# A two-layer convolution block on one Trainium2 core: half of an image's statistics on another engine, small chains cut finer, and outputs one unit later

## The chip, the cores and the metric

The kernel runs on one core of a Trainium2 chip. A core has five engines that matter here, each with its own instruction stream that runs strictly in its own order: TensorE (PE in the profile, with its weight loads as PEld) for matmuls, VectorE (DVE), ScalarE (ACT) and GpSimd (POOL) for elementwise work, and SyncE (SP), which issues all DMAs of this kernel. Data lies in HBM, in the on-chip memory SBUF, or in PSUM, the banks that TensorE writes. The metric is the device time of one execution in microseconds.

## The reference, cut to what matters

The input x is (4, 64, 256, 256), four images of 64 channels. Two layers each add a branch to x. The first layer normalises x by groups (mean and variance of pairs of channels over a whole image) and runs a gated branch; the second normalises the new x and runs two 3x3 convolutions with batch norm.

```python
# layer 0: x = x + L0(gn(x))
h  = gelu(conv3x3(x, c1_w))
xa, k = split(conv1x1(h, c2_w))
xs = gelu(conv_vertical3(conv_horizontal3(xa)))
weights = softmax(xs.mean(axis=(2, 3)) @ gate_w.T)   # one gate per image
mask = the two largest of the three weights, else 0
out = xs
for i in range(3):                                    # ranks 2, 4, 8
    out = out + conv1x1(conv1x1(k, w2) * conv1x1(xs, w1), w3) * mask[i]
y = x + conv1x1(out, proj_w)
# layer 1: y + relu(bn(conv3x3(relu(bn(conv3x3(gn(y)))))) + gn(y))
```

Three things need a whole image before the next step can start: the group norm of x (statistics of x before the first convolution), the gate (the mean of xs before the outputs y), and the group norm of y (statistics of y before layer 1).

## The kernel before

**Tiling.** Two image rows share the 128 partitions with the 64 channels. An image is cut into 16 chunks of 16 rows. The first half of the kernel, the front, works on one chunk at a time; such a step is called a unit. There are 64 units for the four images (`UNITS`), and three more slots to finish. Unit u belongs to image u // 16. The front of a unit: the 3x3 convolution in a form that needs fewer products (differences of input rows on GpSimd and ScalarE, matmuls into the two banks ps_c, "butterflies" on VectorE at L610 to L629, gelu on ScalarE at L637), then the folded 1x1 and vertical taps (matmuls into ps_a, L641 to L671), their horizontal part on ScalarE and VectorE (L677, L683, L686, L689), gelu into xs (L705), the low-rank products (ps_k and ps_q, L712 to L746), and stores of xs and the low-rank product to HBM. ps_a has one bank, so the taps of a half unit must be taken out by L683 and L686 before the next taps may start. ps_c has two banks, freed by the two gelus L637.

**Other work in the units.** Beside the front of its own image, a unit also carries statistics of x of a later image, and outputs y of an earlier one.

- Statistics. A chunk of x is loaded (L403) and reduced. Image 0 is reduced before the units start: half of each chunk by VectorE (`stats_group`, L411, bn_stats over 512 values), half by ScalarE (`stats_piece`, L426: a piece is 1024 values, read twice, once with a shift and once squared, each pass leaving its sum). Images 1, 2 and 3 are reduced by ScalarE alone, two pieces a chunk: image 1 in units 1 to 11, image 2 in units 12 to 27, image 3 in units 28 to 43 (`plan_stats`). Then `stats_end` runs a chain of very small operations: sums on VectorE, a matmul that averages over channels, a mean, a second matmul, a square root on ScalarE, and so on.
- Gate. `gate(b)` is a chain of small operations: a sum, a matmul, a softmax over nine values with an exponential on ScalarE, the choice of the top two by comparisons on VectorE, and the weights `wm` and the bias that the outputs need.
- Outputs. For each of 32 octets of an image (two a unit): load xs, the low-rank product (`ranks`, every second chunk) and x, matmuls into ps_o (bank "p"), add (L848), bn_stats of y (L853), store y. `out_end` then ends the statistics of y with another small chain (L287 and `combine`).

**Order.** The order on all five engines is written out by hand. Each call is put at a step and an order number; `at_slot(u, pos, call)` puts it in slot u, where positions below 6 are its first step and positions from 6 on its second. All calls are then issued in that order. So a call with position 4.1 on VectorE comes after the butterflies of 4.05 and before the output's add (4.3) and L683 (5.2); on ScalarE, 1.52 comes after the second copy out of ps_c (1.4) and before the gelu L705 (1.55), and 4.45 after L677 (4.15). The chains are Python generators: each `yield` ends a part, and each place in a list runs the next part:

```python
e = NCH * b - 4
places = (e, 8.3), (e + 1, 1.25), (e + 1, 1.36), (e + 2, 1.25), (e + 2, 1.36), (e + 2, 1.52), (e + 2, 6.15), (e + 3, 1.25), (e + 3, 1.36)
chain = stats_end(b)
for place in places:
    at_slot(*place, next, chain, None)
```

For image b the gate stands in slots 16(b+1)+1 and 16(b+1)+2, and the outputs start at slot 16(b+1)+3 (`t` in `plan_out`) and take 16 slots: units 19 to 34, 35 to 50, and 51 to 61 for the 22 octets of image 2 that fit. The remaining octets, and all of image 3, are put into the second half, where layer 1's first convolution runs (`plan_out_late`). After that come the second convolution and a last pass that writes the result.

SP issues the DMAs in the same order: in a slot, first the input of a later unit (position 0), the `ranks` loads (0.2), the xs load (0.3), a chunk for the statistics (1.5), the x load for the outputs (2.0), stores of xs (4.7), of the low-rank product (8.1), of y (8.25) and of xs (8.6).

Of the kernel before, what the change touches and what calls it, by code (L numbers as in the profile page):

```python
# [41 lines left out]
def conv_preact_kernel(ctx: ExitStack, tc: tile.TileContext, io, col128, colset, col64):  # L42
# [219 lines left out]
    def combine(mv, n, avg, eps_t, out, name):  # L262
# [5 lines left out]
        nc.vector.tensor_reduce(mean, ps[:, 0:n], AX.X, ALU.add)  # L268
        nc.vector.tensor_scalar(mean, mean, 1.0 / n, None, ALU.mult)
# [155 lines left out]

    def stats_piece(b, n, i, at_sum=None):  # L426
# [29 lines left out]
    def stats_end(b):  # L456

        own = gn1[b] = stat.tile([P, 3], F32, tag="gn1", name=f"gn1_{b}")
        n = 2 if b == 0 else 1
        mv = stat.tile([P, n, 2], F32, tag=f"mv{n}", name=f"mv_x{b}")  # L460
        if b == 0:
            nc.vector.bn_aggr(mv[:, 1, :], flat(st_g.pop(b)))
# [289 lines left out]
    def gate(b):  # L752
# [11 lines left out]
        nc.vector.tensor_copy(lg, ps[:, 0:9])  # L764
        mx = stat.tile([P, 1], F32, tag="s2", name=f"mx_{b}")
# [14 lines left out]
        nc.vector.tensor_scalar(beat[:, 3:6], beat[:, 0:3], -1.0, 1.0, ALU.mult, ALU.add)  # L780
        keep = stat.tile([P, 3], F32, tag="keep", name=f"keep_{b}")
# [202 lines left out]
    with tc.manual_schedule(engines={mybir.EngineType.Activation}):  # L984
        for k in range(NCH):
# [3 lines left out]
            for i in range({0: 0, NCH - 1: 4}.get(k, 2)):  # L989
                stats_group(0, 2 * k - 2 + i if k else 0, k, i)  # L990
            for n in range({0: 2, NCH - 1: 0}.get(k, 1)):
                for i in range(2):
                    stats_piece(0, 2 * k + n if k == 0 else 2 * k + 1, i, k + n if k == 0 else k + 1)
# [13 lines left out]
        for _ in range(7):  # L1007
            next(first_end)
# [31 lines left out]
    def plan_front():  # L1040
# [54 lines left out]
        for b in range(B):  # L1095
            t = NCH * (b + 1)
            if b < B - 1:
                places = (t + 1, 8.3), (t + 2, 1.25), (t + 2, 1.36), (t + 2, 1.52), (t + 2, 6.15), (t + 2, 8.3), (t + 2, 9.06)
# [3 lines left out]
            else:  # L1102
                at_each(((CONV1 + 12 + n, 12.7) for n in (1, 3, 3, 4, 8, 12, 16)), gate(b))
# [11 lines left out]
    def plan_stats(b):  # L1115
# [4 lines left out]
        for k in range(NCH):  # L1120
# [418 lines left out]
```

## Time and profile before

| what | value |
|---|---|
| median of 6 runs | 3035.98 us (3031.72 to 3044.55) |
| profiled execution | 3038.26 us |
| its span in the profile | 3036.4 us |
| front, units 0 to 63 (first ps_c of unit 0 to the end of unit 63) | 63.8 to 1316.4 us |
| bn_stats of image 0 on VectorE, L414 | 32 of 685 ns mean |
| statistics passes on ScalarE, L432 | 112 of 1135 ns and 112 of 1053 ns mean |
| aggregate of y's statistics, L287 | 4 of 1883 ns mean |
| table load on ScalarE | 1283 ns each |

The profile is of one execution. PE, PEld, DVE, ACT, POOL and SP are the engines named above. L683 is line 683 of the kernel below. In a timeline, a row is a group of equal instructions with its start and its length, and in brackets the idle time of the engine before it and what ended it. A window gives for a stretch of time how long each engine was busy, the share of full speed that TensorE's clock was granted, and the share of time that the DMA engines were busy.

### The profile page before, as it was taken

The page shows a single profiled execution, that of the slowest core. Times are in us where ns is not written, and L with a number is a line of the kernel's source. Part 1 is how long each engine was busy: PE and PEld are TensorE (multiplying, and loading weights), DVE is VectorE, ACT ScalarE, POOL GpSimd, SP SyncE. Part 2 cuts the span into 40 slices and gives each one's busy share as a digit, 9 for nine tenths or more (in the row PEclk, how much of TensorE's full clock was granted, in tenths as well). Part 3 has the DMA queues.
Part 4 walks back from the last instruction along what each step waited for, and adds up shares of the span by engine and source line. Part 5 has one row for each costly group of instructions (what it writes and reads, how often), then busy time and mean ns, then how long its engine had stood idle before and what let it go on. Part 6 is the DMA issues. An engine that isn't in the chain of part 4 may idle for free.

```text
span 3036.4 us, 53036 instructions
## 1 busy us (share of the span) xinstructions
PE 2367.6 (78%) x21576; PEld 1506.4 (50%) x21576; DVE 2469.7 (81%) x2793; ACT 2053.7 (68%) x2274; POOL 1674.8 (55%) x1210
## 2 busy tenths in 40 slices
PE   1898899998999999978889999989999999100000
PEld 1444444444544445545556667767888888100000
DVE  5678688888888999968788888979998998876665
ACT  6898887786876555556566677878888888432222
POOL 5888887776777778734435555635555555000000
PEclk9999999999999999999999999999999999555555
DMA  8565479999999889849888898756777764899999
GB/s 343 190 242 223 189 253 369 349 348 344 327 342 328 295 286 326 294 151 319 311 321 334 335 337 324 267 206 234 256 274 262 266 241 139 332 415 421 425 427 411
DMA packets 135572, 915.35 MB, mean 301 GB/s; under 512 B 14944, under 2 KB 15712, under 8 KB 40608
## 3 DMA queue, kind: packets, MB, share of 16 engines
q1 hardware_dynamic: 135328, 911.97, 80.0%
q8 instruction: 169, 2.77, 0.4%
q14 instruction: 75, 0.61, 0.1%
HBM read 573.74 MB, written 338.17 MB: 300 GB/s over the span
## 4 chain that ended last, share of the span: by engine, by line
PE 26%; DMA 19%; DVE 6%; issue 2%; ACT 1%; POOL 1%; SPq 1%; DVEq 0%; POOLq 0%; ACTq 0%
PE ps_h L295 17%; PE ps_h2m L295 6%; DMA y_end<-y_d 5%; DMA out<-h 4%; DMA h<-h_d 4%; PE ps_hm L295 3%; DMA y<-in_xp 2%; DMA xs_in<-xs_d 2%; DVE h L317 1%; DMA yn<-y_d 1%; PE ps_o L492 1%; DVE diff L352 1%; POOL d L342 1%; DVE y L848 1%; DVE odd L361 1%
## 5 line engine op out<-in xcount | busy, mean ns | idle before, releaser
L295 PE MATMUL ps_h<-diff,w_q 128*128 128x512 f32 x3072 | 750.5, 399 | 10.4 <-DVE h L317 10.4
L295 PEld LDWEIGHTS ps_h<-diff,w_q 128*128 128x128 f32 x3072 | 576.4, 189 | 182.9 <-issue 27.2
L492 PE MATMUL ps_c<-v,us 64*64 64x256 f32 x9216 | 548.5, 387 | 41.8 <-DVE ps_c L623 35.8
L342 POOL TENSOR_TENSOR d<-yn 128x1024 f32<-128x1024 f32 x128 | 354.2, 2787 | 317.3 <-DMA yn<-y_d 187.9
L492 PEld LDWEIGHTS ps_c<-v,us 64*64 64x64 f32 x9216 | 363.8, 136 | 199.8 <-DVE ps_c L623 45.3
L492 PE MATMUL ps_a<-h,av 64*64 64x512 f32 x4080 | 389.9, 495 | 38.8 <-DVE t L686 28.6
L342 POOL TENSOR_TENSOR d<-h 128x1024 f32<-128x1024 f32 x127 | 311.8, 2476 | 194.8 <-DVE diff L350 133.3
L317 DVE SCALAR_TENSOR_TENSOR h<-ps_h,scale_w,m 128x1024 f32<-128x1024 f32 x256 | 323.5, 1279 | 65.8 <-PE ps_h L295 49.9
L540 POOL TENSOR_TENSOR x<-x 128x512 f32<-128x512 f32 x256 | 329.9, 1289 | 12.3
L1420 ACT ACTIVATE v<-y_end,shift,gn 128x2048 f32<-128x2048 f32 x64 | 133.8, 2093 | 281.8 <-DMA y_end<-y_d 246.6
L492 PEld LDWEIGHTS ps_a<-h,av 64*64 64x64 f32 x4080 | 155.9, 134 | 308.8 <-issue 204.7
L381 ACT ACTIVATE junk<-h,less_h 128x2048 bf16<-128x2048 f32 (+3 forms) x133 | 256.0, 1925 | 11.1 <-DVE h L317 11.0
L848 DVE SCALAR_TENSOR_TENSOR y<-ps_o,ob,y 128x1024 f32<-128x1024 f32 x128 | 163.8, 1280 | 121.4 <-DMA y<-in_xp 61.7
L1421 DVE SCALAR_TENSOR_TENSOR h<-h,ss,v 128x2048 f32<-128x2048 f32 x64 | 149.8, 2349 | 122.9 <-ACT v L1420 91.6
L683 DVE SCALAR_TENSOR_TENSOR t<-ps_a,m,t 128x1020 f32<-128x1020 f32 x128 | 163.3, 1276 | 104.6 <-ACT t L677 102.6
L677 ACT ACTIVATE t<-ps_a,tap_bias,m 128x1024 f32<-128x1024 f32 x128 | 154.0, 1203 | 103.1 <-PE ps_a L492 102.9
L705 ACT ACTIVATE xs<-t 128x1024 f32<-128x1024 f32 x128 | 134.8, 1054 | 122.6 <-DVE t L689 94.0
L295 PE MATMUL ps_h2m<-odd,w_q 128*128 128x512 f32 x768 | 192.7, 400 | 8.2 <-DVE odd L361 4.4
L295 PE MATMUL ps_hm<-odd,w_q 128*128 128x512 f32 x768 | 193.1, 400 | 4.2 <-ACT k L733 2.4
L352 DVE SCALAR_TENSOR_TENSOR diff<-d,gn,diff 128x1024 fp32r<-128x1024 f32 x128 | 192.1, 1530 | 4.5 <-ACT diff L345 4.5
L345 ACT ACTIVATE diff<-d 128x1024 fp32r<-128x1024 f32 x128 | 135.0, 1055 | 83.3 <-POOL d L342 82.1
L532 POOL TENSOR_TENSOR x<-x,x 128x512 f32<-128x512 f32 x128 | 160.7, 1277 | 43.3 <-ACT x L526 43.3
(226 smaller groups left out, 4322.8 us busy)
## 6 DMA issues: line engine op xcount, KB each, us to landing
h_d<-h SPq DMA_DIRECT2D x114, 1024.0 KB
x<-in_xc SPq DMA_DIRECT2D x64, 1280.0 KB
h<-h_d SPq DMA_DIRECT2D x64, 1152.0 KB
yn<-y_d SPq DMA_DIRECT2D x60, 1152.0 KB
xs_in<-in_xp SPq DMA_DIRECT2D x64, 1024.0 KB
xs_d<-xs SPq DMA_DIRECT2D x128, 512.0 KB
xs_in<-xs_d SPq DMA_DIRECT2D x64, 1024.0 KB
y<-in_xp SPq DMA_DIRECT2D x64, 1024.0 KB
```

Source lines behind the costliest of these rows:

```text
L295: nc.tensor.matmul(ps, wq[w][:, kind, kx, :], t[:, rows, kx : kx + W], start=(j == 0), stop=(j == len(terms) - 1))
L317: nc.vector.scalar_tensor_tensor(h.rearrange("p (e k) w -> p e (k w)", e=2), ps.rearrange("p e k w -> p e (k w)"), w_scale[w], m.unsqueeze ...
L342: engine.tensor_tensor(raw.rearrange("p (g r) w -> p g r w", g=2), *pair, ALU.subtract)
L352: nc.vector.scalar_tensor_tensor(lower, raw, scale, upper.bitcast(F32), ALU.mult, ALU.subtract)
L381: nc.scalar.activation(junk[rows, 0:n], flat(h), AF.Square, bias=less[name][rows], accum_out=total)
L492: last[:] = [nc.tensor.matmul(ps[o, at_out[0] : at_out[1], :], w[i], rhs[i], **flags)]
L532: nc.gpsimd.tensor_tensor(x4[:, j - 1], x_rows(u, j + 2), x4[:, j - 1], ALU.subtract)
L540: nc.gpsimd.tensor_tensor(x[:, r : r + 2], x[:, r + 2 : r + 4], x[:, r : r + 2], ALU.subtract)
L677: nc.scalar.activation(flat(t), flat(ps), AF.Identity, bias=tap_bias, scale=sh[:, 1:2])
L683: nc.vector.scalar_tensor_tensor(t[:, :, 1:W], ps[:, :, 0 : W - 1], sh[:, 0:1], t[:, :, 1:W], ALU.mult, ALU.add)
L848: nc.vector.scalar_tensor_tensor(y, ps.rearrange("p x s w -> p x (s w)"), out_bias[b], y, ALU.add, ALU.add)
L1421: nc.vector.scalar_tensor_tensor(h, h, ss2[:, 0:1], v, ALU.mult, ALU.add)
```

## The change

Four things change.

1. `HALVED = (0, 1)`: image 1's statistics are now split like image 0's. `stats_parts(k)` names for chunk k the groups for VectorE and the pieces for ScalarE. In all 32 bn_stats over 512 values go to VectorE, and 16 of the 32 pieces (two passes each) leave ScalarE. The groups stand at position 4.1 or 6.2 of slots 1 to 11.
2. `combine` has one more part (after its first reduction), and `gate` has two more (after the copy out of PSUM, and after the comparisons).
3. The places of these chains move. The gate's exponential moves from position 1.52 to 4.45, its later parts from 6.15, 8.3 and 9.06 of one slot to 6.05 of that slot and 4.1, 6.05 and 8.3 of the next. In `stats_end` the sums move from 8.3 to 4.1, the mean from 1.36 to 4.1 in part, the square root from 1.52 to 4.45, and the reciprocal from 6.15 to 8.3. `out_end` starts at position 4.1 of the slot after the last outputs instead of 8.3 of that last slot, and ends a slot later.
4. `plan_out` starts an image's outputs one slot later: `t` is 16(b+1)+4. Outputs now stand in units 20 to 35, 36 to 51 and 52 to 62.

The late chains in the second half get an extra place for the extra parts.

```diff
@@ combine
         nc.vector.tensor_reduce(mean, ps[:, 0:n], AX.X, ALU.add)
+        yield
         nc.vector.tensor_scalar(mean, mean, 1.0 / n, None, ALU.mult)
@@ stats
+    HALVED = (0, 1)
+
+    def stats_parts(k):
+
+        groups = [(2 * k - 2 + i if k else 0, k, i) for i in range({0: 0, NCH - 1: 4}.get(k, 2))]
+        pieces = [
+            (2 * k + n if k == 0 else 2 * k + 1, k + n if k == 0 else k + 1)
+            for n in range({0: 2, NCH - 1: 0}.get(k, 1))
+        ]
+        return groups, pieces
+
-        n = NCH if b == 0 else 2 * NCH
+        n = NCH if b in HALVED else 2 * NCH
...
-        n = 2 if b == 0 else 1
+        n = 2 if b in HALVED else 1
...
-        if b == 0:
+        if b in HALVED:
             nc.vector.bn_aggr(mv[:, 1, :], flat(st_g.pop(b)))
@@ gate
         nc.vector.tensor_copy(lg, ps[:, 0:9])
+        yield
         mx = stat.tile([P, 1], F32, tag="s2", name=f"mx_{b}")
...
         nc.vector.tensor_scalar(beat[:, 3:6], beat[:, 0:3], -1.0, 1.0, ALU.mult, ALU.add)
+        yield
         keep = stat.tile([P, 3], F32, tag="keep", name=f"keep_{b}")
@@ plan_front, the gate's places
-                places = (t + 1, 8.3), (t + 2, 1.25), (t + 2, 1.36), (t + 2, 1.52), (t + 2, 6.15), (t + 2, 8.3), (t + 2, 9.06)
+                places = (t + 1, 8.3), (t + 2, 1.25), (t + 2, 1.36), (t + 2, 4.1), (t + 2, 4.45), (t + 2, 6.05), (t + 3, 4.1), (t + 3, 6.05), (t + 3, 8.3)
@@ plan_stats
-            for i in range(2):
+            groups, pieces = stats_parts(k) if b in HALVED else ([], [(2 * k, None), (2 * k + 1, None)])
+            for i, (n, at_sum) in enumerate(pieces):
                 s = slots[k] + i * per / 2
                 first = s - int(s) < 0.5
                 for part in range(2):
-                    at_slot(int(s), ((4.35, 4.4) if first else (5.4, 9.15))[part], stats_piece, b, 2 * k + i, part)
+                    at_slot(int(s), ((4.35, 4.4) if first else (5.4, 9.15))[part], stats_piece, b, n, part, at_sum)
+            for group in groups:
+                s = slots[k] + group[2] // 2 * per / 2
+                at_slot(int(s), 4.1 if s - int(s) < 0.5 else 6.2, stats_group, b, *group)
         e = NCH * b - 4
-        places = (e, 8.3), (e + 1, 1.25), (e + 1, 1.36), (e + 2, 1.25), (e + 2, 1.36), (e + 2, 1.52), (e + 2, 6.15), (e + 3, 1.25), (e + 3, 1.36)
+        places = (e, 4.1), (e + 1, 1.25), (e + 1, 1.36), (e + 1, 4.1), (e + 2, 1.25), (e + 2, 1.36), (e + 2, 4.45), (e + 2, 8.3), (e + 3, 1.25), (e + 3, 1.36)
@@ plan_out
-        t = NCH * (b + 1) + 3
+        t = NCH * (b + 1) + 4
...
-            for place in ((e, 8.3), (e + 1, 1.25), (e + 1, 1.36), (e + 2, 1.25), (e + 2, 1.36), (e + 2, 1.52), (e + 2, 6.15)):
+            for place in ((e + 1, 4.1), (e + 2, 1.25), (e + 2, 1.36), (e + 2, 4.1), (e + 3, 1.25), (e + 3, 1.36), (e + 3, 4.45), (e + 3, 8.3)):
```

More of the change, by code (lines that the diff above doesn't have):

```diff
@@ L988, in conv_preact_kernel @@
                 stats_shift(0)
-            for i in range({0: 0, NCH - 1: 4}.get(k, 2)):
-                stats_group(0, 2 * k - 2 + i if k else 0, k, i)
-            for n in range({0: 2, NCH - 1: 0}.get(k, 1)):
+            groups, pieces = stats_parts(k)
+            for group in groups:
+                stats_group(0, *group)
+            for n, at_sum in pieces:
                 for i in range(2):
-                    stats_piece(0, 2 * k + n if k == 0 else 2 * k + 1, i, k + n if k == 0 else k + 1)
+                    stats_piece(0, n, i, at_sum)
             if k == 5:
@@ L1006, in conv_preact_kernel @@
         first_end = stats_end(0)
-        for _ in range(7):
+        for _ in range(8):
             next(first_end)
@@ L1102, in plan_front @@
             else:
-                at_each(((CONV1 + 12 + n, 12.7) for n in (1, 3, 3, 4, 8, 12, 16)), gate(b))
+                at_each(((CONV1 + 12 + n, 12.7) for n in (1, 3, 3, 3, 4, 8, 12, 12, 16)), gate(b))
         at_slot(1, 1.6, weights1_load)
@@ L1127, in plan_stats @@
                 for part in range(2):
-                    at_slot(int(s), ((4.35, 4.4) if first else (5.4, 9.15))[part], stats_piece, b, 2 * k + i, part)
+                    at_slot(int(s), ((4.35, 4.4) if first else (5.4, 9.15))[part], stats_piece, b, n, part, at_sum)
+            for group in groups:
+                s = slots[k] + group[2] // 2 * per / 2
+                at_slot(int(s), 4.1 if s - int(s) < 0.5 else 6.2, stats_group, b, *group)
         e = NCH * b - 4
-        places = (e, 8.3), (e + 1, 1.25), (e + 1, 1.36), (e + 2, 1.25), (e + 2, 1.36), (e + 2, 1.52), (e + 2, 6.15), (e + 3, 1.25), (e + 3, 1.36)
+        places = (e, 4.1), (e + 1, 1.25), (e + 1, 1.36), (e + 1, 4.1), (e + 2, 1.25), (e + 2, 1.36), (e + 2, 4.45), (e + 2, 8.3), (e + 3, 1.25), (e + 3, 1.36)
         chain = stats_end(b)
@@ L1220, in conv_preact_kernel @@
             if b == B - 2:
-                plan_out_late(b, range(22, NOCT), [CONV1 + 16 + 3 * n for n in range(10)], 13.6, [(CONV1 + n, 12.6) for n in (48, 50, 50, 52, 52, 52, 54)])
+                plan_out_late(b, range(22, NOCT), [CONV1 + 16 + 3 * n for n in range(10)], 13.6, [(CONV1 + n, 12.6) for n in (48, 50, 50, 50, 52, 52, 52, 54)])
         else:
@@ L1224, in conv_preact_kernel @@
             steps = [t + (e - 6 - t) * n // (NOCT - 1) for n in range(NOCT)]
-            plan_out_late(b, range(NOCT), steps, 13.6, [(e - i, 15) for i in (5, 3, 3, 1, 1, 1, -1)])
+            plan_out_late(b, range(NOCT), steps, 13.6, [(e - i, 15) for i in (5, 3, 3, 3, 1, 1, 1, -1)])
         plan_conv1(b)
```

## The prediction

> **What bounds the kernel now.** I read the page's totals first, then the TensorE timeline for a ruler, then windows cut at the units that the change touches, then timelines inside them. A unit is one of the 64 steps of the first half (63.8 to 1316.4 us); it starts where TensorE begins a run of 96 ps_c matmuls.
>
> ```profile
> PE 2367.6 (78%) x21576; PEld 1506.4 (50%) x21576; DVE 2469.7 (81%) x2793; ACT 2053.7 (68%) x2274; POOL 1674.8 (55%) x1210
> ```
>
> No engine is full over the whole, so the stages decide. Columns of the windows: us, busy time of PE, PEld, DVE, ACT, POOL, granted clock, DMA share, GB/s.
>
> ```profile
> 100.88:282.91 182.03, 162.18 (x2326) 85.80 (x2330) 134.87 (x163) 168.53 (x251) 154.47 (x141) 0.97 0.60 217
> ...
> 394.77:416.53 21.76, 17.93 (x249) 9.59 (x246) 18.22 (x28) 18.32 (x25) 17.03 (x16) 0.92 0.92 272
> ...
> 474.52:515.19 40.67, 37.91 (x533) 20.32 (x529) 33.35 (x42) 30.59 (x44) 30.68 (x29) 1.00 0.95 351
> ...
> 717.83:766.05 48.22, 42.05 (x538) 21.02 (x536) 43.88 (x69) 33.75 (x47) 30.65 (x29) 0.93 0.86 318
> 1041.86:1089.79 47.93, 41.48 (x535) 20.65 (x536) 43.64 (x69) 25.10 (x31) 29.63 (x29) 0.93 0.76 258
> ...
> 1128.87:1166.00 37.13, 37.04 (x532) 19.14 (x528) 33.53 (x42) 21.68 (x28) 30.37 (x29) 1.00 0.93 326
> 1277.42:1316.42 39.00, 32.73 (x468) 17.14 (x460) 28.63 (x34) 23.84 (x29) 19.48 (x21) 0.96 0.53 187
> 199.50:202.90 3.40, 3.40 (x40) 2.08 (x36) 3.33 (x3) 2.08 (x4) 2.34 (x3) 0.50 0.00 0
> ```
>
> The reader is to see three regimes. With outputs and no statistics (units 54, 55) TensorE is full: 37.13 a pair, my floor there. With outputs and a later image's statistics (units 21, 22) a pair takes 40.67 at a DMA share of 0.95: transfers bind, 3.5 above the floor. Without outputs (units 2 to 11) a unit takes 18.2, ScalarE busy 168.5 of 182. In units 34, 35 and 50, 51, where a gate chain meets a norm chain, the pair takes 48 and VectorE is busy 44 instead of 33.5.
>
> The floor without outputs is 17.2, between two starts in the TensorE timeline; the third line is a stall in the unit after:
>
> ```profile
> 171.31 5.36 PE L492 MATMUL ps_c<-v,us 64*64 64x256 f32 x96
> ...
> 188.53 5.40 PE L492 MATMUL ps_c<-v,us 64*64 64x256 f32 x96
> ...
> 199.17 4.51 PE L492 MATMUL ps_c<-v,us 64*64 64x256 f32 x48 [2.18 <-DVE ps_c L623]
> ```
>
> In that unit 7 (19.7 us to 208.24) ScalarE works off two statistics passes and `k` (L733, until 193.6) ahead of the copy L605, the butterflies come late, TensorE idles 2.18, and its clock is granted at 0.50 from 199.5 (last window): 48 matmuls take 4.51 instead of 2.82. The gap costs 2.18 + 1.69.
>
> **The change, term by term.** *Statistics of image 1.* ScalarE loses 16 pieces of two passes (1.13 + 1.04, start to start), 34.7 us over units 1 to 11. VectorE gains 32 bn_stats of 0.685 (row L414), 21.9. The gain lies between 0 and 182.0 - 10 x 17.2 = 10.0: units 8, 10 and 16 already stand at 17.2 under 4.7 to 6.9 of passes, so the floor is another chain (the single bank of ps_a: taps, L677, L683, L686, taps). Units 7, 9 and 11 hold most of it, by the cause just shown: I take 9.8. The price: in units 2, 3, 4, 5, 7, 9 and 11 two bn_stats (1.37) stand between L623 and L683. VectorE in unit 16, in unit 12, and in unit 34:
>
> ```profile
> 368.24 0.70 DVE L623 SCALAR_TENSOR_TENSOR ps_c<-d,ps_c 128x512 f32<-128x512 f32 x1
> 369.79 1.28 DVE L683 SCALAR_TENSOR_TENSOR t<-ps_a,m,t 128x1020 f32<-128x1020 f32 x1 [0.86 <-ACT t L677]
> ```
> ```profile
> 299.71 1.27 DVE L441 TENSOR_TENSOR st_sq<-st_sum 128x1 f32<-128x1 f32 x1
> ```
> ```profile
> 742.92 0.14 DVE L779 TENSOR_TENSOR beat<-gate 128x3 f32<-128x3 f32 x1
> 743.09 1.21 DVE L780 TENSOR_SCALAR beat<-beat 128x3 f32<-128x3 f32 x1
> ...
> 746.04 1.88 DVE L287 BATCH_NORM_AGGREGATE mv_y<-st_y 128x2 f32<-128x384 f32 x1
> ...
> 748.66 1.27 DVE L683 SCALAR_TENSOR_TENSOR t<-ps_a,m,t 128x1020 f32<-128x1020 f32 x1
> ```
>
> In unit 16 L683 waits 0.86 for L677, which hides that much of 1.37. Some 0.5 is left, and TensorE's next taps are queued behind L686. Bounds: 0.5 each (3.5) to 1.37 + 1.69 each (21.4), cover gone and clock lost. TensorE's idle there grows from 1.3 to 1.8; 1.32 (unit 6) kept the clock, 2.18 lost it, so I add 1.69 one time in five: 0.85 each, 5.9. The other groups stand behind L629, where VectorE idles 5.24 before 190.59: nothing; 1.37 each without that idle.
>
> *Sums of images 1 to 3, earlier in units 12, 28, 44.* Five small operations, 1.5 by mean rows, 3.5 with waits like 299.71 (298.85 to 302.33); image 1 adds an aggregate (1.02 for image 0, L462). Unit 12: 2.5 - 0.86 and the clock risk, 2.0 (1.0 to 5.3). Unit 44: 1.1. Unit 28: 0.3, the DMA wait of unit 29 covers the rest. GpSimd's edges get their mean a few us later, still a unit ahead.
>
> *Sqrt and Exp move from ahead of L677 to behind it.* With two table loads each is 1.28 + 0.29 + 1.28 = 2.85. Before, they are a 3.10 idle in unit 14 (341.44 - 319.77 = 21.67) and a 2.64 idle in unit 18 (21.76), clock lost in both. Behind L677 they delay L705 and the gelu L637, which frees the bank for the next ps_c. In unit 16 ScalarE idles 0.74 before L705 and the first L637 ends 1.21 before the next unit, so 2.85 - 0.74 - 1.21 = 0.9 is left (0 to 2.85). Unit 14: saves 4.4 to the floor, costs 1.6 (0.9 and the matmul of L276 with its wait, 0.7). Units 18 and 19 (40.2 against 34.4): save 5.8, cost 3.2 (Exp 0.9, L766 and L767 0.5, L779 and L780 0.7, the gate's matmul 0.4, clock risk 0.7). Units 46 and 52 lose 4.0 of such stall (20.79 and 20.33 against 18.57); units 44 to 46 get 2.5 back (1.1, Sqrt 0.9, a matmul), 52 to 54 get 2.9 (L287's 1.88 less 0.5 of cover, two matmuls 0.6, Sqrt 0.9), and 36 to 38 some 0.5, the DMA wait hiding the rest.
>
> *Gate and norm chains spread.* In unit 34 L779 to L799 and L287 are one block from 742.92 to 748.6 ahead of L683; TensorE idles 1.91 and 3.91 and loses the clock twice. Spread, a part is 0.4 to 1.9 against 0.4 to 1.5 of slack at its place. VectorE's sum bounds it below: 33.5 + the 6.9 of the gate that stays in units 50, 51 is 40.4, so 47.93 becomes 40.5 (gain 7.4; from 3, if all six parts cost TensorE 1.3, to 10.8, the floor). Units 34, 35 are held by transfers at 40.7: 48.22 becomes 41.7, 6.5.
>
> *Outputs one unit later.* Unit 19 loses them (counted in its floor), unit 62 gets them: TensorE's idle in units 62, 63 (1.62 and 2.48, both for L623) takes in the two blocks of 1.72, and 39.0 is already above the full pair's 37.13: nothing; 3.4 without that idle. The first differences of conv1 (1295.38) need an output tile whose store is now issued near 1278.8, 16 us of cover. On SP an output's loads and store move along, and the parity flips: two 256 KB loads of `ranks` leave the even slot, where they stand ahead of the `y` load that odd units wait for, and join the odd one. 0.5 MB at 351 GB/s is 1.4 us a pair, over 12 pairs (units 20 to 43) 17 either way. Odd units wait and even ones don't, so I take a small gain, 0.25 a pair: 3.0.
>
> **Sum.** Savings 9.8 + 4.4 + 5.8 + 7.5 (units 34, 35 to 40.7) + 10.8 + 4.0 + 3.0 = 45.3. Costs 5.9 + 2.0 + 1.6 + 3.2 + 0.3 + 1.0 + 3.4 + 0.5 + 2.5 + 2.9 = 23.3. Net minus 22. The profiled execution took 3038.26 (span 3036.4), 2.3 above the median of 3035.98; from the median, **3014 us**. Behind unit 63 only late chains are cut finer.
>
> A rule against the change. L441 took 1.27 above and 0.16 in most of its executions, 1.27 being a GpSimd operation (1.289, L540). The Trainium skill, "SBUF — State Buffer", section "Who interferes with whom", says that a VectorE operation with two SBUF inputs and a reading GpSimd operation exclude each other, the later one waiting out the other. By it each small two-input operation of the sums may wait so wherever it stands, 2 us more in units 12, 28 and 44 each: minus 16 instead of minus 22.
>
> **Rivals.** (A) The relief doesn't reach TensorE in units 2 to 11, and Sqrt and Exp cost as much behind L677: without 3.9, 2.8 and 2.6, minus 12.7, 3023. For it: units 8 and 10 are at the floor already. Against: unit 7's late copy. (B) The parity hurts: odd slots also hold the `low` store; a loss of 17 for the gain of 3 gives minus 2, 3034. For it: the DMA share of 0.95. Against: even units have slack. (C) The parity gives the full 17: 3000. (D) Slower: **VectorE work ahead of L683 becomes the bound.** 18 inserts stand there (7 statistics, 3 sums, 2 aggregates, 6 of gates). If each costs its length and a clock drop, 21.4 + 10.6 + 7.1 + 18.5 = 57.6, with 7 for the rest 64.6 against 45.3: 3055. It decides from 2.1 us an insert, (45.3 - 7) / 18; my sum has 0.9. For it: gaps of 1.62 and 1.91 lost the clock too. Against: the 0.86 that L683 waits.
>
> **How the numbers follow.** Forecast 0.50, own range 3004 to 3024; A 0.14, C 0.10, B 0.11, D 0.15. What a measurement of this kernel tells from no change is 0.2%, 6 us: faster 0.50 + 0.14 + 0.10 = 0.74, same 0.11 (B), slower 0.15 (D). The range 3000 to 3034 takes in C, A and B and leaves D out.
>
> **What would show it.** Units 50, 51 near 40.5 and 34, 35 near 41.7; units 7, 9, 11 under 18.5 at a clock of 1.00; no 3 us gap in units 14 and 18; the `y` wait of odd units shorter and not moved to even ones. Wrong: idle above 1.6 ahead of the ps_a taps in units 2 to 5, L683 right behind bn_stats with windows at 0.50.

## The result and the profile after

The changed kernel takes 3044.49 us in the median of 22 executions (3035.72 to 3057.84), the kernel before 3035.78 in the median of 45 beside it (3027.73 to 3050.56). The ratio is 1.0028, with a 95% interval of 1.0018 to 1.0037. It is slower by 0.3%, where 22 us less were forecast. The profiled execution took 3048.59 us, its span is 3046.8.

The totals by engine moved as the change meant them to: ScalarE 32 us down, VectorE 37 us up.

```profile
PE 2365.1 (78%) x21576; PEld 1497.2 (49%) x21576; DVE 2507.0 (82%) x2826; ACT 2021.3 (66%) x2210; POOL 1675.1 (55%) x1210
```

The windows of the changed kernel at the units that the prediction named: unit 7, units 12, 13, 14, unit 18, units 34 with 35, unit 36, units 50 with 51. The columns are those of the windows of before: us, busy time of PE, PEld, DVE, ACT, POOL, granted clock, DMA share, GB/s.

```profile
189.25:206.76 17.51, 15.64 (x228) 8.22 (x224) 14.88 (x21) 14.81 (x22) 15.53 (x15) 1.00 0.56 189
278.68:303.14 24.46, 19.04 (x244) 9.40 (x240) 21.31 (x30) 13.84 (x19) 17.03 (x16) 0.86 0.60 210
303.14:326.13 22.99, 17.83 (x231) 8.78 (x227) 15.67 (x20) 15.65 (x22) 16.47 (x16) 0.93 0.24 98
326.13:344.92 18.79, 16.39 (x247) 8.27 (x239) 12.21 (x18) 16.68 (x24) 14.55 (x15) 1.00 0.67 237
398.76:417.65 18.89, 16.50 (x250) 9.06 (x244) 16.47 (x24) 17.38 (x25) 16.26 (x16) 1.00 0.65 237
712.45:755.49 43.04, 39.25 (x534) 18.78 (x531) 39.57 (x58) 33.11 (x47) 30.59 (x29) 1.00 0.92 336
755.49:779.08 23.59, 20.62 (x277) 10.93 (x273) 22.74 (x28) 14.78 (x22) 14.96 (x14) 0.93 0.87 324
1037.63:1080.12 42.49, 39.18 (x533) 18.96 (x530) 40.68 (x58) 24.43 (x31) 30.64 (x29) 1.00 0.87 284
```

Unit 7 fell from 19.71 to 17.51 and keeps its clock. Unit 14 lost 2.9 (21.67 before), unit 18 2.9 (21.76), units 34 and 35 went from 48.22 to 43.04 and units 50 and 51 from 47.93 to 42.49. These are the gains that were sought, and they are there. But unit 12 grew from 17.28 to 24.46 and unit 13 from 19.58 to 22.99, with the clock down to 0.86 and 0.93, and unit 36 from 20.05 to 23.59.

**What happens in unit 12.** VectorE of the changed kernel there; in a timeline the columns are start, length, engine, line and operation, and in brackets the idle time before it and what ended it:

```profile
289.56 0.69 DVE L635 SCALAR_TENSOR_TENSOR ps_c<-d,ps_c 128x512 f32<-128x512 f32 x1
290.16 1.01 DVE L474 BATCH_NORM_AGGREGATE mv_x<-st_x 128x2 f32<-128x192 f32 x1
291.09 0.13 DVE L450 TENSOR_REDUCE st_sum<-st_acc 128x2 f32<-128x32 f32 x1
291.26 0.34 DVE L451 TENSOR_SCALAR st_sum<-st_sum 128x2 f32<-128x2 f32 x1
291.63 1.19 DVE L453 TENSOR_TENSOR st_sq<-st_sum 128x1 f32<-128x1 f32 x1
292.86 1.20 DVE L454 TENSOR_TENSOR mv_x<-st_sum,st_sq 128x1 f32<-128x1 f32 x1
293.98 0.14 DVE L455 TENSOR_TENSOR mv_x<-st_sum,shift 128x1 f32<-128x1 f32 x1
294.05 1.27 DVE L695 SCALAR_TENSOR_TENSOR t<-ps_a,m,t 128x1020 f32<-128x1020 f32 x1
```

GpSimd over the same time, and TensorE behind it:

```profile
290.30 1.27 POOL L582 TENSOR_TENSOR v<-x,e 128x512 f32<-128x512 f32 x1
291.53 2.51 POOL L544 TENSOR_TENSOR x<-x,x 128x512 f32<-128x512 f32 x2
```
```profile
286.09 4.07 PE L504 MATMUL ps_a<-h,av 64*64 64x512 f32 x24 [2.05 <-DVE t L698]
...
296.78 4.07 PE L504 MATMUL ps_a<-h,av 64*64 64x512 f32 x24 [3.13 <-DVE t L698]
```

The reader is to see five operations on one or two values per partition that take 3.0 us in all behind an aggregate of 1.01: 3.9 us from the start of the aggregate to that of L695 (L683 before). L453 and L454 take 1.19 and 1.20 where the same kind takes 0.14 in the row after them: each lasts until the GpSimd operation beside it is done. TensorE's next taps wait for L698, 3.13 us, and then run 24 matmuls in 4.07 instead of the 2.38 that they take at full clock. The earlier wait, 2.05 at the beginning of the unit, has another cause, shown in experiment 4. In unit 13 the mean part of the same chain does it again:

```profile
313.54 1.17 DVE L272 TENSOR_SCALAR d_x<-mv_x,gn 128x2 f32<-128x2 f32 x1
314.75 1.20 DVE L273 TENSOR_TENSOR d_x<-d_x 128x2 f32<-128x2 f32 x1
315.98 1.21 DVE L274 TENSOR_TENSOR d_x<-d_x,mv_x 128x2 f32<-128x2 f32 x1
```

L695 follows at 317.11, and TensorE idles 3.5 us.

**What the time is made of.** Unit 63 starts 4.8 us earlier than in the profile before (1291.6 against 1296.4), the last pass 2.6 us earlier (2598.9 against 2601.5), and yet the end is 10.4 us later: the last pass takes 447.9 us instead of 434.9. That pass issues the same transfers in both kernels. So the two profiles alone say neither that the front became slower nor why the median did, and this had to be settled first.

### The profile page after: what moved, and what is told of

Same layout as the page of the kernel before. It is cut to its first block, busy times and chain, and to the rows that moved or that the text cites. A ratio compares the mean times of both kernels' runs of the same rounds, so it can differ in the third digit from the quotient of the medians.

```text
span 3046.8 us, 53014 instructions
## 1 busy us (share of the span) xinstructions
PE 2365.1 (78%) x21576; PEld 1497.2 (49%) x21576; DVE 2507.0 (82%) x2826; ACT 2021.3 (66%) x2210; POOL 1675.1 (55%) x1210
## 4 chain that ended last, share of the span: by engine, by line
PE 27%; DMA 19%; DVE 5%; issue 2%; ACT 1%; SPq 1%; POOL 0%; DVEq 0%; ACTq 0%; POOLq 0%
PE ps_h L296 17%; PE ps_h2m L296 6%; DMA y_end<-y_d 5%; DMA out<-h 4%; DMA h<-h_d 4%; PE ps_hm L296 3%; DMA y<-in_xp 2%; DMA xs_in<-xs_d 2%; PE ps_o L504 1%; DVE h L318 1%; DVE diff L353 1%; DMA yn<-y_d 1%; DVE odd L362 1%; DVE y L862 1%; DMA y_d<-y 1%
## 5 line engine op out<-in xcount | busy, mean ns | idle before, releaser
L504 PE MATMUL ps_c<-v,us 64*64 64x256 f32 x9216 | 537.1, 382 | 36.3 <-DVE ps_c L635 26.3
L504 PEld LDWEIGHTS ps_c<-v,us 64*64 64x64 f32 x9216 | 354.7, 134 | 195.2 <-DVE ps_c L635 35.6
L862 DVE SCALAR_TENSOR_TENSOR y<-ps_o,ob,y 128x1024 f32<-128x1024 f32 x128 | 163.8, 1279 | 99.0 <-DMA y<-in_xp 55.0
L695 DVE SCALAR_TENSOR_TENSOR t<-ps_a,m,t 128x1020 f32<-128x1020 f32 x128 | 163.0, 1274 | 92.1 <-ACT t L689 91.0
L312 ACT ACTIVATE m<-ps_hm,m,scale_w 128x1024 f32<-128x1024 f32 x64 | 77.0, 1204 | 146.5 <-DVE h L318 95.5
```

Source lines behind the costliest of these rows:

```text
L504: last[:] = [nc.tensor.matmul(ps[o, at_out[0] : at_out[1], :], w[i], rhs[i], **flags)]
L695: nc.vector.scalar_tensor_tensor(t[:, :, 1:W], ps[:, :, 0 : W - 1], sh[:, 0:1], t[:, :, 1:W], ALU.mult, ALU.add)
L862: nc.vector.scalar_tensor_tensor(y, ps.rearrange("p x s w -> p x (s w)"), out_bias[b], y, ALU.add, ALU.add)
```

## The experiments

Medians and ratios to the kernel before, each measured beside it on one chip (with fewer loads one execution each, the changed kernel's on another chip):

| kernel | median us (executions) | kernel before, same chip | ratio (95%) |
|---|---|---|---|
| changed, again | 3042.94 (12) | 3036.69 | 1.0024 (1.0012 to 1.0036) |
| statistics half alone | 3039.24 (12) | 3036.69 | 1.0008 (0.9992 to 1.0025) |
| changed without the statistics half | 3033.38 (12) | 3036.69 | 0.9997 (0.9984 to 1.0010) |
| later outputs alone | 3036.94 (12) | 3036.69 | 1.0009 (0.9998 to 1.0021) |
| cut: before / changed | 2643.48 (4) / 2648.82 (4) | 3039.42 | |
| mended | 3029.27 (8) | 3039.42 | 0.9958 (0.9942 to 0.9974) |
| mended, statistics on ScalarE | 3030.29 (11) | 3037.93 | 0.9972 (0.9960 to 0.9984) |
| mended, gate moved too | 3027.60 (7) | 3037.93 | 0.9962 (0.9948 to 0.9976) |
| sums and means alone put back | 3032.12 (12) | 3037.53 | 0.9981 (0.9968 to 0.9994) |
| fewer loads: before / mended | 3029.65 / 3006.82 (1 each) | 3037.93 | |
| fewer loads: changed | 3027.79 (1) | 3037.53 | |

**1. The changed kernel again.** No edit.

> The changed kernel unaltered, profiled a second time. In its first profile unit 63 starts 4.8 us earlier than before the change, conv2 2.6 us earlier, and the last stage is 13 us longer (400 to 407 GB/s against 424 to 427, its large packets late in one cluster per step to the end). Theory SET (the change fixes the pace of the last stage, by what it does to the time at which the stage starts or to what runs ahead of it): the second profile shows the same, last stage 11 to 15 us longer than in the profile before, ratio 1.002 to 1.004. Theory DRAW (the pace of that stage is drawn anew in each execution, whatever the kernel): the stage comes out anywhere between the two lengths, and the ratio, a median over many executions, falls towards 0.999.

Its last pass took 434.4 us and started at 2601.0. Windows of the last pass, changed kernel, first profile and then second:

```profile
2900.00:2950.00 50.00, 0.00 (x0) 0.00 (x0) 31.85 (x14) 12.55 (x6) 0.00 (x0) 0.50 1.01 407
```
```profile
2900.00:2950.00 50.00, 0.00 (x0) 0.00 (x0) 32.19 (x14) 13.87 (x7) 0.00 (x0) 0.50 1.01 427
```

The DMA engines are full in both (1.01), at 407 GB/s in one execution and 427 in the other of the same program. So the pace of this pass is drawn in each execution, as DRAW said. But the ratio stayed at 1.0024, where DRAW expected 0.999: a second cause was missing.

**2. One part at a time.** The statistics half alone is the kernel before with the statistics of the change and nothing else:

```diff
-        if b == 0:
+        if b in HALVED:
             nc.vector.bn_aggr(mv[:, 1, :], flat(st_g.pop(b)))
...
+            for group in groups:
+                s = slots[k] + group[2] // 2 * per / 2
+                at_slot(int(s), 4.1 if s - int(s) < 0.5 else 6.2, stats_group, b, *group)
```

> The kernel before with the statistics half on VectorE alone; all chains and the outputs at their old places. Prediction's reading: units 2 to 11 lose 3 us (as the changed kernel does, not the 9.8 that I forecast), units 34 and 35 stay at about 48 and 50 and 51 at about 48; units 12 and 13 stay at 17.3 and 19.6 because the sums stand at their old place: the front ends 2 to 4 us earlier. SET with the statistics as its cause: the last stage is 11 us or more longer all the same, time 3042 to 3046, ratio 1.002 to 1.004. SET with another cause, or DRAW: last stage as before, 3032 to 3034, ratio 0.9985 to 0.9995.

The changed kernel without it:

```diff
-    HALVED = (0, 1)
+    HALVED = (0,)
```

> The changed kernel without the statistics half on VectorE: chains in more parts at their new places and outputs one unit later, ScalarE keeps all of the second image's statistics. Units 2 to 11 as before the change; units 12 and 13 still long (24 and 23) if the small VectorE operations ahead of L683 cost what they do by waiting for GpSimd, near 17 and 20 if it was the halved statistics that made them long; units 34 and 35 near 43, 50 and 51 near 42.5, so that the front ends about 2 us earlier than before. SET with the chains or the late outputs as its cause: last stage 11 to 15 us longer, ratio 1.002 to 1.004. DRAW, or the statistics as the cause: ratio 0.999 to 1.000.

The later outputs alone, put into the kernel before:

```diff
-        t = NCH * (b + 1) + 3
+        t = NCH * (b + 1) + 4
```

> The kernel before with the outputs of the first three images one unit later and nothing else; gate and norm chains at their old places, the end of the outputs moving with them. If the later outputs alone set units 34, 35, 50 and 51 free, these fall from 48 to 43 and 42.5 a pair, and the front ends about 10 us earlier; if the chains at new places did it, they stay at 48 and only the parity of units 20 to 31 changes, by 0 to 5 us in all. SET with the late outputs as its cause: last stage 11 to 15 us longer, ratio 1.001 to 1.003. Otherwise last stage as before and ratio 0.997 to 0.999.

Lengths of units, from the starts of the ps_c matmuls in each timeline (two profiles of the changed kernel agree within 0.2 in these units):

| units | before | changed | statistics alone | without statistics | later outputs alone |
|---|---|---|---|---|---|
| 2 to 11 | 182.0 | 178.9 | 178.9 | 181.9 | 183.6 |
| 12 | 17.28 | 24.46 | 21.21 | 23.86 | 17.28 |
| 13 | 19.58 | 22.98 | 19.57 | 21.68 | 19.60 |
| 14 | 21.67 | 18.79 | 21.48 | 18.79 | 21.68 |
| 18 and 19 | 40.2 | 38.2 | 40.1 | 38.2 | 39.0 |
| 34 and 35 | 48.2 | 43.0 | 48.2 | 42.5 | 46.7 |
| 50 and 51 | 47.9 | 42.5 | 47.9 | 42.5 | 47.8 |

Units 12 and 13 are long without the halved statistics too, so the chains did it; the halved statistics add 3.9 at unit 12 when they stand alone, which I had not expected at all. Units 34, 35, 50 and 51 were set free by the chains, not by the later outputs. The last passes took 435.8, 433.4 and 441.4, which again fits a draw and no part of the change: the later outputs, with the longest, have a ratio of 1.0009 whose interval holds 1. But the medians of two parts are not as expected: the statistics alone stand at 1.0008, between the ranges of DRAW and SET, with unit 63 no earlier than before (1297.7), and the later outputs alone at 1.0009, where 0.997 to 0.999 was expected. One thing stays open. Without the statistics half the changed kernel is 9.5 us faster in the median on the same chip (3033.38 against 3042.94), though its small operations stand where the changed kernel has them. Its profile shows unit 63 only 1.5 us earlier than the second profile of the changed kernel (1288.4 against 1289.9), but 7.8 earlier than the cut changed kernel of experiment 3 (1296.3), whose time is near its median; 5.7 of the 7.8 lie in units 20 to 33. With one profile of each it can't be told whether that is the price of the statistics half beside the chains or a difference between executions.

**3. The last pass taken away.** Front, both convolutions and 8 of 64 steps of the last pass remain:

```diff
-    steps = chunks[-KEEP:] + chunks[:-KEEP]
+    steps = chunks[-KEEP:][:8]
```

> The kernel before with its last stage ended after 8 of 64 steps: the other 56 outputs are not computed. What is left is the front, conv1, conv2 and 31 us of the last stage. Two theories of why the changed kernel's median is 6 to 9 us longer although its profiles reach the last stage earlier. TAIL: the front, conv1 and conv2 of the changed kernel are 1 to 4 us shorter also in the median, and the last stage is longer by 8 to 12 on average. HEAD: the one profile of the kernel before is a slow execution of its conv1, in the median its last stage starts at 2593 and not at 2601, and the last stage is drawn from the same lot for both kernels. Cut before: TAIL 2636 to 2640, its executions within 4 us; HEAD 2626 to 2631 with executions over 8 us or more.

> The changed kernel with its last stage ended after 8 of 64 steps: the other 56 outputs are not computed. TAIL: median 1 to 4 us below that of the kernel before cut the same way. HEAD: 5 to 9 us above it.

The changed kernel is 5.3 us longer (2648.82 against 2643.48), its executions 2646.0 to 2653.9 against 2643.2 to 2644.1. HEAD had the difference right (5 to 9) and its own account of the kernel before half wrong: that kernel's executions are not spread, they lie within 1 us, and its absolute time was 12 to 17 above what HEAD gave, 12 of which are my slip: the 8 steps that remain end after 43 us and not after 31. The rest of the whole kernels' time is the same: 3036.69 to 3039.42 less 2643.48 is 393 to 396 before, 3042.94 to 3044.49 less 2648.82 is 394 to 396 after. So most of the lost time lies ahead of the last pass, and the first pair of profiles misled: before's front was a long one (unit 63 at 1296.4, 1289.9 in the cut one), after's front a short one (1291.6; 1296.3 in the cut one, 6.3 later than the cut kernel before). This last pair, whose times are near their medians, is the one to take apart below.

**4. The chains put back.** The mended kernel:

```diff
-                at_slot(7 + 3 * i + n, 6.2, next, chain, None)
+                at_slot((7, 15)[i] + n, 6.2, next, chain, None)
...
-        places = (e, 4.1), (e + 1, 1.25), (e + 1, 1.36), (e + 1, 4.1), (e + 2, 1.25), ...
+        places = (e, 8.3), (e + 1, 1.25), (e + 1, 1.36), (e + 1, 1.36), (e + 2, 1.25), ...
...
-            for place in ((e + 1, 4.1), (e + 2, 1.25), (e + 2, 1.36), (e + 2, 4.1), (e + 3, 1.25), ...
+            for place in ((e + 1, 8.3), (e + 2, 1.25), (e + 2, 1.36), (e + 2, 1.36), (e + 3, 1.25), ...
```

> The changed kernel with its small VectorE chains taken from the place ahead of L695 to the places where they stood before: the sums and the output's aggregate at 8.3, the mean parts at 1.36 of the next unit; and the scaling of the w2 weights five units later, at units 15 to 17, so that the three long operations at unit 11 are not there beside the halved statistics. Theory PLACE (small VectorE operations ahead of L695 each wait for a running GpSimd operation and hold up units 12, 13, 36 and 52): unit 12 falls from 24.4 to 17.3 to 18.5, unit 13 from 23.0 to 19.6, units 36 and 52 from 23.3 to 20 to 21, the front ends 10 to 18 us earlier than before the change. Theory DATA (these units wait for something that moves with them, a load or the norm itself): they stay within 1 us of what the changed kernel has. The time: by HEAD 3028 to 3036, by TAIL 3020 to 3035.

Unit 12 fell to 17.21 and unit 13 to 19.59, as PLACE said; unit 52 fell to 21.6, where 20 to 21 was expected, and unit 36 stayed at 23.3: misses, taken up in experiment 6. At 3029.27 us (ratio 0.9958) it beats both kernels. The sums and means alone:

```diff
-        places = (e, 4.1), (e + 1, 1.25), (e + 1, 1.36), (e + 1, 4.1), (e + 2, 1.25), ...
+        places = (e, 8.3), (e + 1, 1.25), (e + 1, 1.36), (e + 1, 1.36), (e + 2, 1.25), ...
```

> The changed kernel with the sums and the mean part of the statistics chain alone back at their old places, 8.3 and 1.36 of the next unit; all else as changed. Theory PLACE: unit 12 falls from 24.4 to about 21.2 (what the halved statistics alone showed there, with the w2 scaling still at unit 11), unit 13 from 23.0 to 19.6, 6 to 7 us of the front; units 36 and 52 stay at 23.3. If that lead lasts to the end the time is 6 us below the changed kernel's, ratio 1.000 to 1.001 to the kernel before; if the transfers of units 20 to 44 take it back, ratio 1.001 to 1.0025.

Unit 12 took 21.22 and unit 13 19.58, just as expected, and the time fell more than expected: 0.9981, so that this one list of places turns the change from slower into slightly faster. The same three operations at their old place, VectorE in unit 13 of this kernel:

```profile
306.63 0.39 DVE L272 TENSOR_SCALAR d_x<-mv_x,gn 128x2 f32<-128x2 f32 x1
307.05 0.16 DVE L273 TENSOR_TENSOR d_x<-d_x 128x2 f32<-128x2 f32 x1
307.24 0.16 DVE L274 TENSOR_TENSOR d_x<-d_x,mv_x 128x2 f32<-128x2 f32 x1
```

They take 0.7 in all here and 3.6 in the changed kernel. What is left in unit 12 of this kernel, 4 us, stands at its beginning; VectorE from the end of unit 11 on:

```profile
277.12 1.56 DVE L253 TENSOR_SCALAR mset<-mset 128x768 f32<-128x768 f32 x1
278.72 1.50 DVE L254 TENSOR_SCALAR mset<-mset 128x768 f32<-128x768 f32 x1
280.14 1.27 DVE L415 BATCH_NORM_STATS2 st_x<-xs_in 128x6 f32<-128x512 f32 x2
...
282.52 0.68 DVE L420 BATCH_NORM_STATS2 first<-xs_in 128x6 f32<-128x512 f32 x1
...
283.52 1.27 DVE L695 SCALAR_TENSOR_TENSOR t<-ps_a,m,t 128x1020 f32<-128x1020 f32 x1
```

The last two groups of the halved statistics stand at the end of unit 11 behind the scaling of the w2 weights, and push all that follows into unit 12. The mended kernel, whose w2 scaling is elsewhere, has unit 12 at 17.21.

**5. Fewer transfers.** Half of the statistics loads of the third and fourth image are left out, in the kernel before, the mended and the changed one:

```diff
     def stats_load(b, k, tag, bufs):
+        if b > 1 and k % 2:
+            x_in[b, k] = x_in[b, k - 1]
+            return
```

> The kernel before with half of the statistics loads of the third and fourth image left out (an odd chunk's statistics are taken from the chunk before it, so the numbers differ): about 1 MB less a pair in units 12 to 43. Theory GIVEN BACK (in units 24 to 44 a pair is bound by its transfers, so what the mended kernel gains before, it gives back there): its pairs of units 24 to 31 fall from 40.2 to 40.8 us to 37.2 to 38.5. Theory ENGINES (the pairs are bound by VectorE and TensorE and the waits are theirs): they stay within 1 us of 40.5.

> The mended kernel with the same loads left out. Cut or whole, the mended kernel stood 8.5 us ahead of the kernel before at unit 20 and 12.5 at unit 24, but only 7.5 at unit 34 and 6.7 at unit 63. GIVEN BACK: with the transfers relieved in both, it keeps its lead: 8 to 10 us ahead at unit 20 and 7 to 11 still at unit 34, pairs of 37.2 to 38.5. ENGINES: its lead shrinks between units 24 and 34 as before, by 4 us or more.

> The changed kernel itself with half of the statistics loads of the third and fourth image left out, as in the two runs before. GIVEN BACK: with the transfers relieved, its outputs one unit later bring in units 20 to 33 what they bring the mended kernel there, 12 to 13 us, against the kernel before with the same loads left out; with 10 us lost at units 12 and 13 and 4 at units 44 and 45 it still starts unit 63 some 12 us (8 to 16) earlier, and runs 3016 to 3024. ENGINES (what holds the units 20 to 33 of the changed kernel are its own engines, and the mended kernel's lead there is owed to its chains): it stands within 4 us of the kernel before at unit 63, 3026 to 3032.

Windows of units 20 to 23 and 24 to 27, two pairs each, first with all transfers: the cut kernel before, the cut changed kernel, the mended kernel.

```profile
434.23:512.54 78.31, 75.18 (x1060) 38.40 (x1056) 66.52 (x83) 61.08 (x87) 61.63 (x57) 1.00 0.97 348
512.54:592.92 80.38, 75.42 (x1060) 38.84 (x1056) 66.60 (x83) 60.87 (x87) 61.35 (x57) 1.00 0.94 355
```
```profile
437.60:511.91 74.31, 74.15 (x1057) 38.60 (x1061) 66.26 (x86) 61.15 (x87) 60.45 (x57) 1.00 0.99 354
511.91:594.43 82.52, 75.48 (x1061) 37.94 (x1057) 67.09 (x83) 60.77 (x87) 61.22 (x57) 1.00 0.94 345
```
```profile
425.76:500.07 74.31, 74.14 (x1056) 38.16 (x1060) 66.29 (x86) 61.16 (x87) 60.49 (x56) 1.00 0.98 355
500.07:581.00 80.93, 75.23 (x1061) 37.88 (x1057) 67.19 (x83) 60.69 (x87) 61.26 (x57) 1.00 0.95 348
```

Then with fewer: the kernel before, the mended kernel, and the changed kernel with units 28 to 31 as well.

```profile
434.93:513.18 78.25, 75.28 (x1061) 38.97 (x1057) 66.87 (x83) 61.02 (x87) 61.74 (x57) 1.00 0.94 325
513.18:593.21 80.03, 75.43 (x1060) 38.92 (x1056) 66.59 (x83) 60.97 (x87) 61.44 (x57) 1.00 0.91 331
```
```profile
427.57:501.89 74.32, 74.15 (x1056) 38.57 (x1060) 66.30 (x86) 61.15 (x87) 60.48 (x56) 1.00 0.95 336
501.89:576.17 74.28, 74.10 (x1060) 38.55 (x1056) 67.12 (x83) 60.71 (x87) 61.30 (x57) 1.00 0.93 355
```
```profile
437.08:511.38 74.30, 74.14 (x1056) 38.15 (x1060) 66.28 (x86) 61.17 (x87) 60.52 (x56) 1.00 0.95 332
511.38:585.65 74.27, 74.09 (x1060) 38.20 (x1056) 67.12 (x83) 60.76 (x87) 61.32 (x57) 1.00 0.93 357
585.65:670.98 85.33, 78.06 (x1066) 39.06 (x1062) 75.87 (x100) 64.63 (x91) 63.35 (x60) 0.98 0.89 312
```

For the kernels with later outputs GIVEN BACK holds. With all transfers they run units 20 to 23 at TensorE's floor of 37.15 a pair, and in units 24 to 27 fall back to 40.5 (mended) and 41.3 (changed, cut; 39.3 and 39.2 in the two profiles of the whole changed kernel); with fewer transfers they stay at 37.14, and the mended kernel's lead over the kernel before grows from 7.4 us at unit 20 to 20.1 at unit 34 and 28.2 at unit 63, where with all transfers it was 7.5 at unit 34 and 6.7 at unit 63 (cut kernel before); a lead of 7 to 11 at unit 34 was expected. For the kernel before, GIVEN BACK was wrong: its pairs stay at 39.1 and 40.0. Its odd units still wait for the load of `y` with fewer loads, as VectorE does in unit 25:

```profile
544.42 1.28 DVE L851 SCALAR_TENSOR_TENSOR y<-ps_o,ob,y 128x1024 f32<-128x1024 f32 x1 [3.48 <-DMA y<-in_xp]
```

The changed kernel led by 4.6 us at unit 63, where I had expected 8 to 16, and its one time, 3027.79, lies in the range that ENGINES gave. Its units 20 to 27 are at the floor, but units 28 and 29 take 23.5 and 21.4 (mended 19.1 and 19.8): the third image's sums, ahead of L698 in unit 28 (this kernel has three lines more, so its L698 is L695 above),

```profile
596.51 1.20 DVE L456 TENSOR_TENSOR st_sq<-st_sum 128x1 f32<-128x1 f32 x1
597.74 1.21 DVE L457 TENSOR_TENSOR mv_x<-st_sum,st_sq 128x1 f32<-128x1 f32 x1
598.88 1.30 DVE L458 TENSOR_TENSOR mv_x<-st_sum,shift 128x1 f32<-128x1 f32 x1
```

three operations on one value that take 3.7 us. With all transfers most of the same loss hides in the wait for them (unit 28: 22.40 changed, 22.69 mended; both units: 43.8 to 44.4 changed, 42.5 mended). Between changed and mended, with fewer loads, it comes to 10.6 in units 12 and 13, 6.0 in 28 and 29, 1.5 in unit 37, 4.5 in 44 to 46 and 2.0 in 52 and 53: 24.6 us, of 23.7 that lie between the two at unit 63. That is the price of the places at 4.1, with the 4 us of the w2 scaling in it.

**6. Two more versions of the mended kernel.** All statistics of the second image on ScalarE again:

```diff
-    HALVED = (0, 1)
+    HALVED = (0,)
```

> The mended kernel with all of the second image's statistics on ScalarE again: what the halved statistics are worth once the small chains are out of the way. Units 2 to 11 as in the kernel before, 3 to 4 us longer than in the mended kernel, unit 12 at 17.3. If that lead lasts, the time is 3 us above the mended kernel's (ratio 0.9965 to 0.9975); if it is given back to the transfers of units 20 to 44, the two are equal within 1.5 us (ratio 0.9955 to 0.9965).

0.9972 is inside the first range, 0.9965 to 0.9975; but the intervals of the two kernels overlap, so the statistics half is worth 1 us by the medians, 4 by the ratios, and is not told from nothing. And the gate's last parts, split once more:

```diff
-                places = ..., (t + 2, 6.05), (t + 3, 4.1), (t + 3, 6.05), (t + 3, 8.3)
+                places = ..., (t + 2, 6.05), (t + 2, 8.3), (t + 3, 1.36), (t + 3, 1.36), (t + 3, 6.05)
```

> The mended kernel with the gate's last parts taken from the end of a unit: the comparison half a unit earlier, the kept weights and their row at 1.36 of the next unit, and the scaled matrix (two operations of 1.23 us at the end of unit 35, which run on into unit 36 ahead of L695) half a unit earlier. If these were what holds unit 36 at 23.3 and unit 52 at 21.6 to 23.3, unit 36 falls to 20 to 21.5 without unit 35 (20.8) growing as much, and units 18 and 19 stay at 18.9 and 19.3 or lose 1; the time is 2 to 5 us below the mended kernel's. If VectorE has no room in unit 35 either, what unit 36 loses unit 35 gains, and the time is the mended kernel's within 1.5 us.

What holds unit 36 of the changed kernel, VectorE at its beginning:

```profile
758.75 1.23 DVE L809 TENSOR_TENSOR wm<-row,pw 128x256 f32<-128x256 f32 x1
759.91 1.23 DVE L813 TENSOR_TENSOR ob<-row,m 128x1 f32<-128x1 f32 x1
761.06 1.27 DVE L695 SCALAR_TENSOR_TENSOR t<-ps_a,m,t 128x1020 f32<-128x1020 f32 x1
```

With these parts moved, units 35 and 36 went from 20.8 and 23.3 to 19.8 and 22.9, unit 52 from 21.6 to 18.8, and unit 19 from 19.3 to 18.0. Unit 36 fell less than expected (20 to 21.5). Its first taps are freed all the same: TensorE in the mended kernel, then with the gate moved, and VectorE there:

```profile
759.10 4.04 PE L504 MATMUL ps_a<-h,av 64*64 64x512 f32 x24 [2.90 <-DVE t L698]
```
```profile
754.09 2.33 PE L504 MATMUL ps_a<-h,av 64*64 64x512 f32 x24
```
```profile
763.17 1.28 DVE L863 SCALAR_TENSOR_TENSOR y<-ps_o,ob,y 128x1024 f32<-128x1024 f32 x1 [4.58 <-DMA xs_d<-xs]
```

The idle time and the slow taps are gone, but later in the unit the output's add waits 4.58 us for a transfer, which takes most of it back. The ratio, 0.9962, can't be told from the mended kernel's.

## Why the prediction was wrong

The cut pair of profiles (unit 63 at 1289.91 before, 1296.25 after) against the terms of the sum, in us:

| units | forecast | cut pair |
|---|---|---|
| 0 and 1 | 0 | +0.4 |
| 2 to 11 | -3.9 | -3.0 |
| 12 and 13 | +2.0 | +10.5 |
| 14 to 19 | -5.4 | -4.5 |
| 20 to 33 | -1.5 | +1.0 |
| 34 and 35 | -6.5 | -3.7 |
| 36 to 38 | +0.5 | +5.9 |
| 39 to 43 | -1.2 | -3.7 |
| 44 to 49 | +0.3 | +2.6 |
| 50 and 51 | -7.4 | -5.6 |
| 52 to 61 | +1.1 | +4.8 |
| 62 | 0 | +1.7 |
| sum | -22.0 | +6.3 |

Rows differ in how well they repeat. In the two profiles of the whole changed kernel against that of the whole kernel before, units 12 and 13 come out at +10.6 and +10.5, 44 to 49 at +2.6 twice and 52 to 61 at +4.8 and +4.2, but units 20 to 33 at -7.4 and -6.2 and unit 62 at 0.

**Right in mechanism and nearly in size.** ScalarE's relief (units 7 and 11 at 17.5 and full clock; unit 9, forecast under 18.5, stayed at 19.9); two bn_stats ahead of L695, forecast at 0.85 in each of seven units, cost 1.06 and 0.87 in units 2 and 4 and next to nothing in the others; Sqrt and Exp behind the taps (no 3 us gap in units 14 and 18); the gate and norm chains in units 34, 35, 50 and 51 (43.0 and 42.5 where 41.7 and 40.5 were forecast), where the single parts showed that the chains did it. That units 2 to 11 come out at -3.0 for -3.9 is luck in part: the relief brought 5 and not 9.8, the bn_stats cost 2 and not 5.9.

**The step that failed** is the term "Sums of images 1 to 3, earlier in units 12, 28, 44" and its like: small operations ahead of L683 priced by mean rows. It gave unit 12 2.0 (1.0 to 5.3), units 44 to 46 2.5, units 52 to 54 2.9, units 36 to 38 0.5, and the mean part in unit 13 nothing. The runs showed in its place that at position 4.1 two or three operations of each of these chains end with a GpSimd operation, some 1.2 us each, since GpSimd works without a break just there; and that the delay is long enough for TensorE to lose its clock in units 12 and 13 both. Putting the sums and means back moved the ratio from 1.0024 to 0.9981. In the table these places are units 12 and 13, 36 to 38, 44 to 49 and 52 to 61: 20 of the 28 us between forecast and measurement in this pair. The medians don't divide as the units do: the kernel without the halved statistics keeps these places and still stands at 0.9997, so the whole loss showed only with both, and how they share it stays open. Two smaller items of the same step: the groups behind L629, priced at nothing, cost 4 at unit 12 with the sums at their old place, since the idle of unit 7 that was to hide them was taken for that of unit 11, where the w2 scaling fills it; and the gate's last part, moved to the end of unit 35, runs on into unit 36.

**The rule that I weighed against the row.** The Trainium skill, "SBUF — State Buffer", section "Who interferes with whom", was cited for minus 16 instead of minus 22. The runs side with the rule: L453 takes 0.16 or 1.19 and L273 0.16 or 1.20, depending on the place, and L454 waits at its old place too (1.14 in the mended kernel). It was even too mild as I used it, because I charged the sums for it and not the mean part, and not the clock that follows. The same section counts `tensor_scalar` among the operations that can take the shared ports, and L272, a TENSOR_SCALAR, took 0.39 at its old place and 1.17 at the new.

**The outputs one unit later.** "Odd units wait and even ones don't, so I take a small gain, 0.25 a pair." Half of the mechanism was as described: odd units lost most of their wait for `y`. But the wait moved to even units, which the prediction's own sign excluded: in the cut changed kernel L862 waits 4.0 us in unit 24 and 4.6 in unit 26. With fewer transfers the gain is 2.4 a pair (158.3 before against 148.6 in units 20 to 27), more than the 1.4 a pair behind rival C. With all transfers units 20 to 23 gain 4.0 in the cut pair and units 24 to 33 lose 5.0, with the DMA engines at 0.94 and the chain of units 28 and 29 in it; the later outputs alone, without that chain, gain 4.3 and lose 3.7 against the cut kernel before. The small number was luck as far as its own reason goes; what kept it small is another thing that I had read, the 40.67 of a pair that is bound by transfers.

**Rival D** came nearest: VectorE work ahead of L683 as the bound. It decides from 2.1 us an insert by its own account; the inserts that mattered were not its seven groups of statistics but the chains' parts, and it ended at 3055 instead of 3044. B and C are both half true: with all transfers most of the gain is given back, with fewer it is larger than C's. A fell: the relief did reach TensorE, and Sqrt and Exp cost little.

**The basis.** The sum was made against one profiled execution. The fronts of the kernel before, whole and cut, differ by 6.5 us at unit 63, and last passes of one program by 13.5, more than half of the forecast change. This did not turn the sign, but it hid it in the first comparison of profiles.

## What to carry to other kernels

A small operation is priced by the place where it goes, not by its mean row: look what GpSimd does at that very moment, and what waits behind it. Where a stretch is bound by transfers, a gain ahead of it lasts only up to the next full stretch; leave some transfers out once to see what the engines' part is worth. And before two profiles are compared, cut off the part that is drawn anew in each execution, or profile the same kernel twice.

## What the runs showed of the hardware

- The fronts of all fifteen traces (63 to 1300 us) hold 825 TENSOR_TENSOR and TENSOR_SCALAR operations of VectorE on one or two values per partition. The 291 that began with no GpSimd operation running took 0.22 us at most. All 246 that took 0.3 us or more began under a running GpSimd operation and ended within 0.07 us after the end of one; 189 of them took 0.9 to 1.3.
- Not every kind is held up. Of those that began with more than 0.3 us of a GpSimd operation ahead of them, all 30 TENSOR_SCALAR on 128x2 were (L272, 1.17), and none of the 117 on 128x1 (0.22 at most). TENSOR_REDUCE (L450, 0.12 to 0.13 on 32 values in three kernels) and the aggregate L474 (1.01 in each) were not.
- After idle stretches of TensorE of 2.05 and 3.13 us, 24 matmuls took 4.07 us instead of 2.38. The length of the idle alone doesn't decide: in the kernel before, 48 matmuls took 4.51 us after an idle of 1.62 (at 1287.5) and 2.82 after one of 2.48 (at 1307.3).
- The last pass, which keeps the DMA engines full, ran at 398 to 427 GB/s over 50 us, in executions of one program. Its 8192-byte packets take 309 ns in the median in both profiles of the changed kernel; in the last 48 of its 64 steps the first profile has 480 packets over 450 ns, in about one cluster a step, and the second 61. What starts or ends such clusters isn't settled.
- From the first to the 49th of conv1's 64 chunks (starts of VectorE's `odd<-yn`) the profiles take 580.5 (before) to 592.5 us, 588.9 in the mended kernel, as a rule longer in the kernels with a short front. Some of a front's gain is lost there: the mended kernel leads by 13.2 us at unit 63, 4.8 at the 49th chunk and 5.0 at the last pass, against the profile before. This was not taken further.
